# Perceiver kernel: context features copied out raw and rectified later, exponential's table loaded behind the logarithm, three feature buffers

## The chip, the cores and the metric

One Trainium2 chip, one core. The metric is the device time of one execution in microseconds (us), lower is better. All data is float32 unless said otherwise.

## What is computed

The reference runs four layers of a small perceiver on a latent array `x` of 2 batches x 256 tokens x 256 features, with a context `ctx` of 2 x 4096 x 256. The change touches two cross attentions to the context (layers 0 and 1) and a third one (layer 3). Cut to what matters:

```
# layers 0 and 1: masked softmax attention to the context, 16 heads of 16
q, k, v = heads(h @ Wq), heads(ctx @ Wk), heads(ctx @ Wv)
x = x + merge(softmax(mask(q @ k.T / 4)) @ v)

# layer 3: linear attention on "focused" features
def focus(x, factor):
    x = abs(where(x >= 0, x, 0.01 * x)) + 1e-6
    return softmax(log(x) * factor, axis=-1) * x.mean(axis=-1)
def sparsify(x):          # within each head of 16 features, keep the 11 largest
    return x * (rank(x) < 11)
k = sparsify(focus(ctx @ Wk.T)); q = sparsify(focus(h @ Wq.T))
y = (q @ (k.T @ v)) / (q @ k.mean(axis=1) + 1e-6)
```

The focused features of the context, `sparsify(focus(ctx @ Wk.T))`, and their sums `k.T @ [ctx, 1]` do not depend on `x`. The kernel works them out early, in the gaps of the two context attentions: batch 0 within layer 0's, batch 1 within layer 1's.

## The kernel before

Class `ContextAttention` does one context attention. Its work is cut into 8 units (`UNITS`: a batch and a group of 4 heads), each of `PER` = 16 rounds. The loop in `attend` (L944) runs over rounds `g` and issues, in this order: `first_scores` (L1070: scores of a unit against a half of 512 keys and 128 queries, of which VectorE takes the maximum at L1088); the round's *fill* (L962), some work chosen ahead by the planner; a few steps of VectorE's ranking of features (L963 to L967); `scores` (L1094) of the unit before, with its maximum already subtracted, in two PSUM pairs that ScalarE turns into weights by two exponentials (L1114); `weigh` (L1117), PE's product of the weights of one round earlier with the values; and the steps of a chunk's weighing (L976). PE, VectorE and ScalarE run strictly in the order of the program (`manual_schedule`), so whatever is issued first on an engine is in front of what follows. PSUM holds three pairs for the scores (`sc=3`), one bank for all fills (`mm=1`) and one for the weighed sum (`acc=1`).

A fill is one of: keys (L991), values (L1033), one or two tiles of 128 tokens of the context's features (`Focus.project`, L721), half of the sums of a chunk (`add_up`, L745), a unit's shift of the queries or its normalization. Class `Focus` (L584) treats the context in 8 chunks of 4 tiles:

- `project` multiplies a tile with the weights into the PSUM bank and calls `magnitudes` (L604) for each tile. That runs two Relus on ScalarE, straight from PSUM, with scales 1 and -0.01, into the chunk's buffer `y` (tile `fy`, of which there are 2) and into `low` (1 buffer), each with the row's total as an accumulator. POOL adds the two (L611).
- `weigh` (L613) is a generator of five parts: a logarithm of the whole chunk (L618) and POOL's product with the factor (L619); the maximum on VectorE (L621); four exponentials in two parts (L624); small factors (L629 to L632). Logarithm and exponential use different tables of ScalarE; the compiler puts a table load ahead of an activation whose table isn't there. Relu and copy need none.
- `sparsify` (L640) ranks the features by 15 comparisons, 47 parts in all, the first ones long (960 elements a partition) and the last ones short (64), and ends with POOL's scaling by the factors (L665).
- `add_up` multiplies the chunk with the context's tokens on PE.

`plan` (L835) decides all of it ahead, step by step, by a list `todo` of (deadline, earliest, which). In each round without a fixed fill it takes the first that is ready in order of deadline. Features come in pairs of tiles where time is short (`pressed`, L895). Chunk `kc`'s features may be planned once the sums of `kc - 2` are. When the last tile of a chunk is planned in round g, its weighing is put at rounds g+1, g+3, g+4, g+5 and g+6 (L920), and round g+2 is marked in `logs`: nothing but sums, or work that is due, is planned there (L886), so that round is often empty. The ranking may begin at g+7. `credit` paces the ranking by VectorE's estimated free time in a round (2.0 us, or 2.75 with a fill of eight matmuls, less what is `taken`), by the costs at L634.

In layer 3, `l3_xattn` (L1776) calls `magnitudes` (L1814), with a scale by row, and `weigh` (L1816) for the query's features, outside of any plan.

Of the kernel before, what the change touches and what calls it, by code (L numbers as in the profile page):

```python
# [19 lines left out]
F32 = mybir.dt.float32  # L20
BF16 = mybir.dt.bfloat16
I32 = mybir.dt.int32
AF = mybir.ActivationFunctionType
# [3 lines left out]
P = 128  # L27
# [556 lines left out]
class Focus:  # L584
# [19 lines left out]
    def magnitudes(self, pool, y, total, t, ps, scales=(1.0, -0.01)):  # L604


        nc = self.nc
        low = pool.tile([P, D], F32, tag="low", name="low", bufs=1)
        for i, (out, scale) in enumerate(zip((y[:, t, :], low), scales)):
            nc.scalar.activation(out, ps, AF.Relu, scale=scale, accum_out=total[:, i, t : t + 1])  # L610
        nc.gpsimd.tensor_tensor(y[:, t, :], y[:, t, :], low, ALU.add)  # L611

    def weigh(self, y, total, factor):  # L613


        nc = self.nc
        top, norm = (self.net.sm(NT, name=n, tag=n) for n in ("f_top", "f_norm"))
        nc.scalar.activation(y, y, AF.Ln, bias=self.eps)  # L618
        nc.gpsimd.tensor_scalar(y, y, self.power[:, 0:1], 1.0, ALU.mult, ALU.mult)  # L619
# [12 lines left out]
        nc.vector.tensor_tensor(factor, factor, norm, ALU.mult)  # L632
# [61 lines left out]


    def start(self, b, pool):
        self.b, self.pool, self.chunks, self.ctx, self.weighing = b, pool, [], [], []
# [23 lines left out]
    def project(self, kc, first, n=1):  # L721

        net, nc = self.net, self.nc
        if first == 0:
            y = self.pool.tile([P, NT, D], F32, name="fy", tag="fy")
# [15 lines left out]
        for i in range(n):  # L741
            self.magnitudes(self.pool, y, total, first + i, ps[:, i * D : (i + 1) * D])
        yield

    def add_up(self, kc, m):  # L745

# [14 lines left out]
class ContextAttention:  # L761
# [73 lines left out]
    def plan(self):  # L835
# [24 lines left out]
        for kc in range(NKC):  # L860
            first = 5 + 31 * kc // 2
            todo += [(first + 2 * t + 4, first + t, ("features", kc, t)) for t in range(NT)]
            todo += [(first + 30 + m, first + 14, ("sums", kc, m)) for m in range(ND)]
        for j in range(self.begun, n * NKC // 2):


# [15 lines left out]
        ranked, at = 0, 0  # L882

        def ready(g, deadline, earliest, which):
            kind, kc, *_ = which
            if earliest > g or (g in logs and kind != "sums" and deadline > g):  # L886
                return False
            if kind == "keys":

                return kinds.get(g - 1) != kind or deadline <= g  # L890
            if kind == "features":
                return kc < 2 or not any(w[:2] == ("sums", kc - 2) for _, _, w in todo)
            return kind != "sums" or over.get(kc, g) + 1 < g

        def pressed(g):  # L895
# [6 lines left out]
        for g in range(STEPS):  # L902
            room = short
            t = None if g in fills else next((t for t in todo if ready(g, *t)), None)
            if t is not None:
                todo.remove(t)
                kind, *which = t[2]
                kinds[g] = kind
                assert t[0] >= g or kind in ("features", "sums"), (g, t)
                fills[g] = make[kind](*which)  # L910
                if kind == "features":
                    kc, tile = which
                    if tile + 1 < NT and pressed(g):
                        todo.remove(next(t for t in todo if t[2] == ("features", kc, tile + 1)))
                        fills[g] = focus.project(kc, tile, 2)
                        room, tile = full, tile + 1
                    if tile == NT - 1:


                        for behind in (0, 2, 3, 4, 5):  # L920
                            self.weighings.setdefault(g + 1 + behind, []).append(kc)
                        logs.add(g + 2)
                        taken[g + 3] += 1.22
                        taken[g + 6] += 0.65
                        begin[kc] = g + 7
                else:
                    room = full
                    taken[g] += 0.42 * (kind == "sums")
            if g < PER:
                room = 0.5  # L930
            if g >= last + 1:
                room = 2.2
            credit = min(credit, 0.5) + room - taken[g]
# [10 lines left out]
    def attend(self, vpool, ppool, fpool):  # L944
# [12 lines left out]
        for g in range((n + 1) * PER + LAG + 2):  # L957
# [9 lines left out]
                run(rankings[kc], 1)  # L967
            if 0 <= second < n * PER:
                self.scores(second // PER, second % PER)
            if 0 <= second - 1 < n * PER:  # L970
                self.weigh((second - 1) // PER, (second - 1) % PER)
            if g in self.done:
# [1229 lines left out]
```

## Time and profile before

| | us |
|---|---|
| median of three runs | 2561.95 (2557.09 to 2562.78) |
| the profiled execution, whole | 2563.84 |
| its span, first to last instruction | 2562.1 |
| PE, VectorE (DVE), ScalarE (ACT), POOL busy | 2343.6, 1558.8, 1054.6, 355.6 |
| rounds with first and second scores, layer 0 | from about 90 to 650 |
| the same, layer 1 | from about 1022 to 1586 |
| table loads at L618 (17) and at L1114 (14), each | 1.28 |

The profile is one execution. A line of the timeline gives the start in us, the duration, the engine, the line of the kernel, the operation, what it writes and reads, the shapes, and in brackets the idle time of the engine ahead of it and what ended that. PEld is PE's loading of weights. Float32 matmuls count as two each. An ACTIVATION_READ_ACCUMULATOR follows each ScalarE instruction that writes a total. Lines of DVE, ACT or POOL in a group are followed by their count (x2).

### The profile page before, as it was taken

How to read it: one execution, taken by the hardware profiler on the slowest of the kernel's cores; microseconds unless marked ns; L12 is line 12 of the kernel's file. 1: busy time of each engine (PE TensorE's matmuls, PEld its weight loads, DVE VectorE, ACT ScalarE, POOL GpSimd, SP SyncE). 2: the span in 40 equal slices, each digit the busy share in tenths (PEclk: the TensorE clock that was granted, in tenths of full speed). 3: DMA queues.
4: the chain of work that ended last, by engine and by line, in shares of the span. 5: the costliest groups of instructions: out<-in, count | busy, mean ns of one | idle time of the engine just before them, and what ended most of it. 6: DMA issues, size and time to landing. Idle time of an engine off the chain costs nothing.

```text
span 2562.1 us, 42559 instructions
## 1 busy us (share of the span) xinstructions
PE 2343.6 (91%) x17006; PEld 1247.1 (49%) x17014; DVE 1558.8 (61%) x2702; ACT 1054.6 (41%) x1830; POOL 355.6 (14%) x523
## 2 busy tenths in 40 slices
PE   7999999999998579999999999989999996789998
PEld 3454545544544354544555544554448453345453
DVE  4968897779546468888878878243331254335252
ACT  2455555555616132555555555431131252223141
POOL 3000010000034612100011000000020031003030
PEclk9999999999989789999999999988999897898989
DMA  5432223231010133232222220202222100000100
GB/s 191 137 97 80 93 88 94 71 107 43 10 55 17 47 107 108 91 95 95 94 88 82 83 76 26 81 14 61 87 89 88 42 18 14 33 21 12 56 12 21
DMA packets 97797, 174.40 MB, mean 68 GB/s; under 512 B 15120, under 2 KB 63888, under 8 KB 96704
## 3 DMA queue, kind: packets, MB, share of 16 engines
q1 hardware_dynamic: 97600, 171.68, 20.7%
q8 instruction: 135, 2.21, 0.4%
q14 instruction: 62, 0.51, 0.1%
HBM read 154.25 MB, written 0.59 MB: 60 GB/s over the span
## 4 chain that ended last, share of the span: by engine, by line
PE 79%; DVE 10%; ACT 5%; issue 3%; POOL 2%; DMA 1%; SPq 0%; ACTq 0%; DVEq 0%; POOLq 0%
PE s L1080 11%; PE s L1104 10%; PE attn_acc L1128 9%; PE v_ps L180 6%; PE proj L180 6%; PE k_ps L1001 4%; DVE mx L1088 3%; PE kc_sum L180 2%; PE expert L180 2%; PE s L180 2%; PE c_acc L1666 2%; PE f_ps L180 2%; PE ffn_ps L180 2%; PE s L1402 2%; PE o L411 1%
## 5 line engine op out<-in xcount | busy, mean ns | idle before, releaser
L1088 DVE TENSOR_REDUCE mx<-s 128x2 f32<-128x1024 f32 x512 | 603.5, 1220 | 206.3 <-PE s L1080 203.6
L1114 ACT ACTIVATE p<-s 128x1024 f32<-128x1024 f32 x512 | 496.3, 1021 | 237.9 <-PE s L1104 235.8
L1104 PE MATMUL s<-xa_q,xa_k 32*128 32x256 f32 x4096 | 339.0, 403 | 22.9 <-DVE mx L1088 20.8
L1080 PE MATMUL s<-xa_k,xa_q 32*128 32x512 f32 x2048 | 345.3, 639 | 7.6 <-ACT p L1114 3.6
L1104 PEld LDWEIGHTS s<-xa_q,xa_k 32*128 32x128 f32 x4096 | 211.8, 184 | 160.5 <-issue 98.5
L1128 PE MATMUL attn_acc<-p,xv 128*32 128x256 f32 x4096 | 277.1, 387 | 0.9 <-ACT p L1114 0.9
L1080 PEld LDWEIGHTS s<-xa_k,xa_q 32*128 32x128 f32 x2048 | 116.4, 183 | 128.9 <-issue 58.7
L654 DVE TENSOR_TENSOR ge<-fy 128x960 bf16<-128x960 f32 (+14 forms) x240 | 172.9, 720 | 6.2
L1128 PEld LDWEIGHTS attn_acc<-p,xv 128*32 128x32 f32 x4096 | 107.5, 109 | 132.2 <-issue 85.5
L611 POOL TENSOR_TENSOR fy<-fy,low 128x256 f32<-128x256 f32 x64 | 50.4, 787 | 793.1 <-ACT low L610 793.1
L656 DVE TENSOR_TENSOR rank<-rank,ge 128x960 bf16<-128x960 bf16 (+14 forms) x240 | 111.4, 464 | 6.0
L658 DVE TENSOR_TENSOR rank<-rank,ge 128x960 bf16<-128x960 bf16 (+14 forms) x240 | 105.6, 440 | 2.7
L387 POOL TENSOR_SCALAR p<-p,r 128x128 f32<-128x128 f32 (+1 forms) x192 | 82.7, 444 | 140.2 <-DVE r L383 80.0
L1048 ACT COPY xv<-v_ps 128x512 f32<-128x512 f32 x64 | 37.6, 588 | 142.8 <-PE v_ps L180 133.0
L368 ACT ACTIVATE p<-p,top 128x256 f32<-128x256 f32 (+1 forms) x128 | 57.1, 447 | 42.7 <-DVE top L356 40.2
L180 PE MATMUL f_ps<-f_wk,f_ctx 128*128 128x256 f32 x256 | 70.0, 401 | 1.2 <-ACT low L610 1.2
L1001 PE MATMUL k_ps<-ctx_k,w_L0x_wq 128*64 128x512 f32 x256 | 65.1, 615 | 2.6 <-DMA ctx_k<-in_ctxT 2.2
L1666 PE MATMUL c_acc<-pT,ctx_n 128*128 128x256 f32 x256 | 63.1, 392 | 4.2 <-ACT pT L1639 3.0
L180 PEld LDWEIGHTS f_ps<-f_wk,f_ctx 128*128 128x128 f32 x256 | 44.1, 189 | 46.8 <-issue 27.3
L233 ACT ACTIVATE sq<-xc 128x512 f32<-128x512 f32 x24 | 14.7, 630 | 125.8 <-DVE xc L232 125.8
L180 PE MATMUL v_ps<-w_L0x_wv,ctx_v 128*128 128x256 f32 x256 | 63.8, 392 | 0.8 <-ACT k_dense L1014 0.8
L180 PE MATMUL kc_sum<-f_tok,fy 128*128 128x257 f32 x256 | 64.2, 393 | 0.0
(458 smaller groups left out, 3365.1 us busy)
## 6 DMA issues: line engine op xcount, KB each, us to landing
ctx_k<-in_ctxT SPq DMA_DIRECT2D x128, 512.0 KB
ctx_v<-in_ctxT SPq DMA_DIRECT2D x64, 256.0 KB
xa_k<-k_dense SPq DMA_DIRECT2D x512, 32.0 KB
f_ctx<-in_ctxT SPq DMA_DIRECT2D x32, 256.0 KB
f_tok<-in_ctx SPq DMA_DIRECT2D x16, 512.0 KB
ctxT<-in_ctxT SPq DMA_DIRECT2D x16, 512.0 KB
ctx_n<-in_ctx SPq DMA_DIRECT2D x16, 512.0 KB
xa_k<-key_masks SPq DMA_DIRECT2D x128, 8.0 KB
```

Of the source, the lines that this page charges most:

```text
L180: self.nc.tensor.matmul(out, lhsT=lhsT, rhs=rhs, start=i == 0, stop=i == len(pairs) - 1)
L387: nc.gpsimd.tensor_scalar(p[:, j, :nk], p[:, j, :nk], r[:, j : j + 1], 1.0, ALU.mult, ALU.mult)
L654: nc.vector.tensor_tensor(ge[:, :, :n], w[:, :, :n], w[:, :, P - n :], ALU.is_ge)
L656: nc.vector.tensor_tensor(rank[:, :, P - n :], rank[:, :, P - n :], ge[:, :, :n], ALU.add)
L658: nc.vector.tensor_tensor(rank[:, :, :n], rank[:, :, :n], ge[:, :, :n], ALU.subtract)
L1001: nc.tensor.matmul(ps[i * HR : (i + 1) * HR, :], lhsT=self.wk[:, d, c * HR : (c + 1) * HR], rhs=ctx[:, d, :], start=d == 0, stop=d == ND - 1,)
L1080: nc.tensor.matmul(pairs[i // 2][:, i % 2, :], lhsT=self.q[u][rows, qt * P : (qt + 1) * P], rhs=k[rows, :], start=True, stop=True,)
L1088: nc.vector.tensor_reduce(mx[:, qt, 2 * i : 2 * i + 2, kc], sc, AX.X, ALU.max)
L1104: nc.tensor.matmul(pairs[i // 2][:, i % 2, kk * S : (kk + 1) * S], lhsT=k[rows, at], rhs=self.q[u][rows, :], start=True, stop=True,)
L1114: nc.scalar.activation(p, sc, AF.Exp, scale=DH**-0.5)
L1128: nc.tensor.matmul(self.acc[i * HP : (i + 1) * HP, :S], lhsT=v[:, 2 * k2 + kk, at : at + HP], rhs=ps[i // 2][:, i % 2, kk * S : (kk + 1) * S],
L1666: nc.tensor.matmul(accs[m], lhsT=of[:, (k + i) % (KC // P), m * P : (m + 1) * P], rhs=pT[:, i, :], start=k + i == 0, stop=k + i == KT - 1,)
```

## The change

`project` copies the raw products of its one or two tiles from PSUM into `y` by one ScalarE copy, and notes the tiles in `taken`. A new method `magnitudes_of_taken` runs the Relus from `y`, `low` first and then `y` in place; `attend` calls it behind `scores`, so behind the round's exponentials. `low` has two buffers and `fy` three; features of chunk `kc` may be planned once the sums of `kc - 3` are. In `weigh`, an exponential of one column (`ready`) stands directly behind the logarithm. The planner no longer sets a chunk's weighing at once: it keeps the chunk in `waiting` until sums are planned in some round, or until the ranking of the chunk before is over or has 30 of its parts planned; from there the distances of the weighing's parts and the ranking are as before. The sums' deadline is half a round earlier.

```
@@ -605,9 +605,9 @@
         nc = self.nc
-        low = pool.tile([P, D], F32, tag="low", name="low", bufs=1)
-        for i, (out, scale) in enumerate(zip((y[:, t, :], low), scales)):
-            nc.scalar.activation(out, ps, AF.Relu, scale=scale, accum_out=total[:, i, t : t + 1])
+        low = pool.tile([P, D], F32, tag="low", name="low", bufs=2)
+        for i, out in ((1, low), (0, y[:, t, :])):
+            nc.scalar.activation(out, ps, AF.Relu, scale=scales[i], accum_out=total[:, i, t : t + 1])
         nc.gpsimd.tensor_tensor(y[:, t, :], y[:, t, :], low, ALU.add)
     def weigh(self, y, total, factor):
@@ -616,6 +616,9 @@
         nc = self.nc
         top, norm = (self.net.sm(NT, name=n, tag=n) for n in ("f_top", "f_norm"))
         nc.scalar.activation(y, y, AF.Ln, bias=self.eps)
+
+        ready = self.net.sm(1, name="ready", tag="ready")
+        nc.scalar.activation(ready, self.eps, AF.Exp)
         nc.gpsimd.tensor_scalar(y, y, self.power[:, 0:1], 1.0, ALU.mult, ALU.mult)
         yield
         nc.vector.tensor_reduce(top, y, AX.X, ALU.max, negate=True)
@@ -694,7 +697,7 @@
     def start(self, b, pool):
-        self.b, self.pool, self.chunks, self.ctx, self.weighing = b, pool, [], [], []
+        self.b, self.pool, self.chunks, self.ctx, self.weighing, self.taken = b, pool, [], [], [], []
         self.loads = iter([(kc, i) for kc in range(NKC) for i in range(2)])
         self.tokens = pool.tile([P, NT, D + 1], F32, name="f_tok", tag="f_tok", bufs=1)
@@ -722,7 +725,7 @@
         net, nc = self.net, self.nc
         if first == 0:
-            y = self.pool.tile([P, NT, D], F32, name="fy", tag="fy")
+            y = self.pool.tile([P, NT, D], F32, name="fy", tag="fy", bufs=3)
             total = net.sm(2, NT, name="f_total", tag="f_total")
             factor = net.sm(NT, name="f_factor", tag="f_factor")
             self.chunks.append((y, total, factor))
@@ -738,9 +741,15 @@
             ctx = self.ctx[kc * 2 + t // 2]
             at = slice(t % 2 * P, (t % 2 + 1) * P)
             net.matmuls(ps[:, i * D : (i + 1) * D], [(ctx[:, d, at], self.wk[:, d, :]) for d in range(ND)])
-        for i in range(n):
-            self.magnitudes(self.pool, y, total, first + i, ps[:, i * D : (i + 1) * D])
+
+        nc.scalar.copy(y[:, first : first + n, :], ps[:, : n * D].rearrange("p (t d) -> p t d", t=n))
+        self.taken += [(y, total, first + i) for i in range(n)]
         yield
+
+    def magnitudes_of_taken(self):
+        for y, total, t in self.taken:
+            self.magnitudes(self.pool, y, total, t, y[:, t, :])
+        self.taken = []
     def add_up(self, kc, m):
@@ -860,7 +869,7 @@
         for kc in range(NKC):
             first = 5 + 31 * kc // 2
             todo += [(first + 2 * t + 4, first + t, ("features", kc, t)) for t in range(NT)]
-            todo += [(first + 30 + m, first + 14, ("sums", kc, m)) for m in range(ND)]
+            todo += [(first + 29.5 + m, first + 14, ("sums", kc, m)) for m in range(ND)]
         for j in range(self.begun, n * NKC // 2):
@@ -879,7 +888,17 @@
         make = dict(keys=self.project_keys, values=self.project_values, features=focus.project, sums=focus.add_up)
         self.weighings, self.rankings, costs = {}, {}, focus.costs()
         begin, over, logs, credit = {}, {}, set(), 0.0
-        ranked, at = 0, 0
+        ranked, at, waiting = 0, 0, []
+
+        def take_logs(g):
+
+            kc, _ = waiting.pop(0)
+            for behind in (0, 2, 3, 4, 5):
+                self.weighings.setdefault(g + behind, []).append(kc)
+            logs.add(g + 1)
+            taken[g + 2] += 1.22
+            taken[g + 5] += 0.65
+            begin[kc] = g + 6
         def ready(g, deadline, earliest, which):
             kind, kc, *_ = which
@@ -889,7 +908,7 @@
                 return kinds.get(g - 1) != kind or deadline <= g
             if kind == "features":
-                return kc < 2 or not any(w[:2] == ("sums", kc - 2) for _, _, w in todo)
+                return kc < 3 or not any(w[:2] == ("sums", kc - 3) for _, _, w in todo)
             return kind != "sums" or over.get(kc, g) + 1 < g
         def pressed(g):
@@ -915,21 +934,19 @@
                         fills[g] = focus.project(kc, tile, 2)
                         room, tile = full, tile + 1
                     if tile == NT - 1:
-
-
-                        for behind in (0, 2, 3, 4, 5):
-                            self.weighings.setdefault(g + 1 + behind, []).append(kc)
-                        logs.add(g + 2)
-                        taken[g + 3] += 1.22
-                        taken[g + 6] += 0.65
-                        begin[kc] = g + 7
+                        waiting.append((kc, g))
                 else:
                     room = full
                     taken[g] += 0.42 * (kind == "sums")
+
+                    if kind == "sums" and waiting and waiting[0][1] < g - 1:
+                        take_logs(g - 1)
             if g < PER:
                 room = 0.5
             if g >= last + 1:
                 room = 2.2
+            if waiting and waiting[0][1] < g and (ranked == waiting[0][0] or ranked + 1 == waiting[0][0] and at >= 30):
+                take_logs(g)
             credit = min(credit, 0.5) + room - taken[g]
             while ranked < NKC and begin.get(ranked, STEPS) <= g and credit > 0.3:
                 self.rankings.setdefault(g, []).append(ranked)
@@ -967,6 +984,7 @@
                 run(rankings[kc], 1)
             if 0 <= second < n * PER:
                 self.scores(second // PER, second % PER)
+            focus.magnitudes_of_taken()
             if 0 <= second - 1 < n * PER:
                 self.weigh((second - 1) // PER, (second - 1) % PER)
             if g in self.done:
```

More of the change, by code (lines that the diff above doesn't have):

```diff
@@ L607, in magnitudes @@
         nc = self.nc
-        low = pool.tile([P, D], F32, tag="low", name="low", bufs=1)
-        for i, (out, scale) in enumerate(zip((y[:, t, :], low), scales)):
-            nc.scalar.activation(out, ps, AF.Relu, scale=scale, accum_out=total[:, i, t : t + 1])
+        low = pool.tile([P, D], F32, tag="low", name="low", bufs=2)
+        for i, out in ((1, low), (0, y[:, t, :])):
+            nc.scalar.activation(out, ps, AF.Relu, scale=scales[i], accum_out=total[:, i, t : t + 1])
         nc.gpsimd.tensor_tensor(y[:, t, :], y[:, t, :], low, ALU.add)
@@ L618, in weigh @@
         nc.scalar.activation(y, y, AF.Ln, bias=self.eps)
+        ready = self.net.sm(1, name="ready", tag="ready")
+        nc.scalar.activation(ready, self.eps, AF.Exp)
         nc.gpsimd.tensor_scalar(y, y, self.power[:, 0:1], 1.0, ALU.mult, ALU.mult)
@@ L696, in start @@
     def start(self, b, pool):
-        self.b, self.pool, self.chunks, self.ctx, self.weighing = b, pool, [], [], []
+        self.b, self.pool, self.chunks, self.ctx, self.weighing, self.taken = b, pool, [], [], [], []
         self.loads = iter([(kc, i) for kc in range(NKC) for i in range(2)])
@@ L724, in project @@
         if first == 0:
-            y = self.pool.tile([P, NT, D], F32, name="fy", tag="fy")
+            y = self.pool.tile([P, NT, D], F32, name="fy", tag="fy", bufs=3)
             total = net.sm(2, NT, name="f_total", tag="f_total")
@@ L740, in project, with magnitudes_of_taken @@
             net.matmuls(ps[:, i * D : (i + 1) * D], [(ctx[:, d, at], self.wk[:, d, :]) for d in range(ND)])
-        for i in range(n):
-            self.magnitudes(self.pool, y, total, first + i, ps[:, i * D : (i + 1) * D])
+        nc.scalar.copy(y[:, first : first + n, :], ps[:, : n * D].rearrange("p (t d) -> p t d", t=n))
+        self.taken += [(y, total, first + i) for i in range(n)]
         yield
+    def magnitudes_of_taken(self):
+        for y, total, t in self.taken:
+            self.magnitudes(self.pool, y, total, t, y[:, t, :])
+        self.taken = []
     def add_up(self, kc, m):
@@ L862, in plan @@
             todo += [(first + 2 * t + 4, first + t, ("features", kc, t)) for t in range(NT)]
-            todo += [(first + 30 + m, first + 14, ("sums", kc, m)) for m in range(ND)]
+            todo += [(first + 29.5 + m, first + 14, ("sums", kc, m)) for m in range(ND)]
         for j in range(self.begun, n * NKC // 2):
@@ L881, in plan, with take_logs @@
         begin, over, logs, credit = {}, {}, set(), 0.0
-        ranked, at = 0, 0
+        ranked, at, waiting = 0, 0, []
+        def take_logs(g):
+            kc, _ = waiting.pop(0)
+            for behind in (0, 2, 3, 4, 5):
+                self.weighings.setdefault(g + behind, []).append(kc)
+            logs.add(g + 1)
+            taken[g + 2] += 1.22
+            taken[g + 5] += 0.65
+            begin[kc] = g + 6
         def ready(g, deadline, earliest, which):
@@ L891, in ready @@
             if kind == "features":
-                return kc < 2 or not any(w[:2] == ("sums", kc - 2) for _, _, w in todo)
+                return kc < 3 or not any(w[:2] == ("sums", kc - 3) for _, _, w in todo)
             return kind != "sums" or over.get(kc, g) + 1 < g
@@ L917, in plan @@
                     if tile == NT - 1:
[L920 to L925, printed above, removed]
+                        waiting.append((kc, g))
                 else:
@@ L928, in plan @@
                     taken[g] += 0.42 * (kind == "sums")
+                    if kind == "sums" and waiting and waiting[0][1] < g - 1:
+                        take_logs(g - 1)
             if g < PER:
@@ L932, in plan @@
                 room = 2.2
+            if waiting and waiting[0][1] < g and (ranked == waiting[0][0] or ranked + 1 == waiting[0][0] and at >= 30):
+                take_logs(g)
             credit = min(credit, 0.5) + room - taken[g]
@@ L969, in attend @@
                 self.scores(second // PER, second % PER)
+            focus.magnitudes_of_taken()
             if 0 <= second - 1 < n * PER:
```

## The prediction

> **What bounds the kernel now.** I read the chain of waits first, then the two stretches in which the changed code runs, then single steps in the timeline.
>
> ```profile
> PE 79%; DVE 10%; ACT 5%; issue 3%; POOL 2%; DMA 1%; SPq 0%; ACTq 0%; DVEq 0%; POOLq 0%
> ```
>
> ```profile
> 90.00:650.00 560.00, 545.35 (x5116) 278.94 (x5116) 459.79 (x645) 306.08 (x458) 49.29 (x68) 1.00 0.26 84
> 1022.00:1586.00 564.00, 548.73 (x5132) 280.93 (x5132) 458.74 (x643) 303.73 (x458) 48.59 (x68) 0.99 0.26 83
> ```
>
> The second fence gives the two middle stretches of the context attentions (start:end, length, then busy us of PE, PE's loads, DVE, ACT and POOL). ScalarE is busy for 306 of 560 us, so it has room on average. It matters only where its queue is momentarily late. A step is the distance between the first L1080 matmuls of successive rounds in the timeline, and it comes in two kinds. With a fill of eight matmuls (keys, values, sums) it takes 5.24 to 5.31 us and PE is full. With one feature tile, a transpose of the maxima or no fill it takes 4.52 us whatever PE has to do: the first scores, their maximum, the second pair of scores and the weighing follow each other through three PSUM pairs. So a single feature tile costs no more than an empty step, and I look for gain only in steps above these two values.
>
> The first such kind is a step with two feature tiles:
>
> ```profile
> 265.68 1.15 PE L1104 MATMUL s<-xa_q,xa_k 32*128 32x256 f32 x16
> 265.83 0.38 ACT L610 ACTIVATE fy<-f_ps 128x256 f32<-128x256 f32 x1 [2.28 <-issue]
> 266.81 0.89 POOL L611 TENSOR_TENSOR fy<-fy,low 128x256 f32<-128x256 f32 x1 [26.70 <-ACT low L610]
> 267.15 1.37 DVE L654 TENSOR_TENSOR ge<-fy 128x768 bf16<-128x768 f32 x1
> 267.74 0.38 ACT L610 ACTIVATE low<-f_ps 128x256 f32<-128x256 f32 x1 [0.70 <-POOL fy L611]
> 268.11 1.93 ACT L1114 ACTIVATE p<-s 128x1024 f32<-128x1024 f32 x2
> 268.26 0.52 PEld L180 LDWEIGHTS sums<-den,a 128*128 128x128 f32 x4 [0.92 <-ACT low L610]
> ```
>
> Four Relus run ahead of the exponentials, the last one waits 0.70 us for the one `low` tile, the exponentials start at 268.11, and PE waits 0.92 us because the Relus still hold the single mm bank. The second kind follows a logarithm:
>
> ```profile
> 152.32 1.15 ACT L618 ACTIVATE fy<-fy,eps 128x1024 f32<-128x1024 f32 x1
> 154.36 1.28 ACT L1114 ACT_TABLE_LOAD   x1 [0.90 <-PE s L1104]
> 155.66 1.94 ACT L1114 ACTIVATE p<-s 128x1024 f32<-128x1024 f32 x2
> ...
> 223.14 1.15 ACT L618 ACTIVATE fy<-fy,eps 128x1024 f32<-128x1024 f32 x1
> 224.30 1.28 ACT L1114 ACT_TABLE_LOAD   x1
> 225.60 1.94 ACT L1114 ACTIVATE p<-s 128x1024 f32<-128x1024 f32 x2
> ...
> 229.76 0.59 ACT L1048 COPY xv<-v_ps 128x512 f32<-128x512 f32 x1 [2.23 <-PE v_ps L180]
> ```
>
> At 154.36 (a step with sums) the load of exponential's table waits 0.90 us for scores that it doesn't need. At 224.30 (an empty step) it already stands directly behind the logarithm. The step after takes 6.58 and 6.49 us, against 5.30 normally: 1.2 to 1.3 us are lost, the time that the exponentials were late. The copy at 229.76 shows 2.23 us of idle ScalarE behind a step's exponentials.
>
> **What the Trainium skill says.** "ScalarE: Activation LUTs", section "What ACT_TABLE_LOAD costs", gives 1283 ns for a load, 186 ns + 0.833 ns an element for an ACTIVATE with immediates, 93 ns more for each pointer operand, and an overlap of 93 ns between neighbours. The trace agrees: 1283 ns, and 384 ns for the Relu of 256 elements (399 by the formula). It adds a drain of about 1380 ns to a load; here the logarithm starts 0.02 us behind its load, so I count none. Its section "Table sets: the hidden batching unit" has relu and copy in every set; no load stands at L610, so Relus and copies may go anywhere. "GPSIMD Engine Reference", section "1. Specifications", says that POOL contends with DVE instructions that have two SBUF inputs: the `ge` of 768 at 267.15, beside POOL's add, took 1.37 us, against 0.96 us at 657.93 with POOL idle.
>
> **The change, part by part** (minus is faster).
>
> *Copy and late Relus, two tiles.* ScalarE now makes one copy of 128x512 (0.59 us, the row of L1048) before the exponentials. It ends at 265.83 + 0.59 = 266.42; the scores would allow the exponentials at 266.93 (1.25 us behind L1104's start, as at 317.40 and 318.64). So it is hidden, as a value fill's is. The Relus move behind the exponentials and read SBUF. No row shows that: the floor is 0.38 us (PSUM, L610), the ceiling 0.51 (L624, SBUF with a pointer bias). I take 0.41, four are 1.65 us and fit into the 2.23 us idle; at the ceiling 2.04 still do. POOL's add moves along; its queue has nothing urgent. Steps with two tiles and a denominator in the middle stretches take 6.35, 6.51, 6.48, 6.34, 6.51, 6.47 us; the same with keys takes 5.78 (at 181.96, 511.05). That is 0.57 + 0.73 + 0.70 + 0.56 + 0.73 + 0.69 = 3.98. Two more, at 103.21 and 1035.27, delay their successors to 6.27 and 6.22 against 5.30: 1.89. Sum **-5.9**. A single tile gains nothing: its step is at 4.52 with the Relus in it.
>
> *First phase* (no second scores). Here the Relus hold the mm bank:
>
> ```profile
>   PEld sums L180: 6.1, 6
>   PEld f_ps L180: 4.3, 4
> ```
>
> The first row is already in the 5.9. Of the 4.3 us in the second, VectorE's maxima, which run nearly without a gap from 53.9 to 67.9 and from 991.2 to 1000.5, let through about what DVE idles: 0.9 in the first attention (of 1.04 us idle at 63.24), 0.3 in the second. **-1.2**.
>
> *The small exponential.* The same instruction at L955:
>
> ```profile
> L955 ACT ACTIVATE ready<-eps x2: 203/204/204, 26.4 to 965.2; 128x1 f32<-128x1 f32 x2
> ```
>
> In an empty step it removes nothing and adds 0.11 to 0.20 us in front of the exponentials; I take 0.15. In a step with sums the load moves from 154.36 to the logarithm's end at 153.47, and the exponentials from 155.66 to about 154.95: -0.7.
>
> *The log's place and three buffers.* A log now waits until the ranking before it has 30 of its 47 parts planned, or is over, or until sums come. Followed by hand with the planner's own costs, 30 parts are 20.2 of 26.1 us of ranking. Chunk 1 finds its ranking over: same place, beside sums, in both layers. For chunks 2, 3, 4 and 7 the ranking has 20 to 29 parts when the tiles are done, so the logs go one to three steps later; chunk 5 goes one later, and its step, which had sums at 463.38, becomes empty; chunk 6 stays. I find no log that moves onto sums: those of the chunk before come only when its ranking is over, and those of two before are done by then. So in each layer 5 logs with work behind them lie in empty steps, and the log of chunk 7, with empty steps behind it, costs nothing now (4.55 at 623.03). That gives 10 x 0.15 = **+1.5** and 2 x 0.7 = **-1.4**. Moving an empty step changes nothing in the sum, since the number of steps and fills is fixed. The third buffer only allows the delay. Rankings of chunks 2 to 4 shift by two or three steps, and nothing waits for them; sums of the last chunk come three or four steps later in the tail, where the last ranking would end near 682 and POOL's factors near 684, against PE reaching those sums near 687: hidden by 3 us. The half step in the sums' deadline only changes ties. No DMA and no SP instruction is added; a feature load goes out when its tile is planned, as before.
>
> *The query's features (L1814)* share the code. `low` comes first and needs `low_rstd`, ready 0.21 us after `rstd`: **+0.2**. The small exponential stands there behind a load that POOL and DVE cover (2150.10 to 2152.59).
>
> Sum: -5.9 - 1.2 + 1.5 - 1.4 + 0.2 = **-6.8 us**. The profiled execution took 2563.84 us, 1.7 more than its span, and would take 2557.0. It lies 1.9 us above the median of the three runs, 2561.95, so the forecast is 2561.95 - 6.8 = 2555.2, written as 2555.
>
> **Rivals.**
> 1. *Logs meet sums.* If the planner puts the ten logs beside sums after all, each loses the 0.15 and gains 0.7: 8.5 us more, 2547. For it: the diff has a branch for it. Against: the order of the rankings, above.
> 2. *Cover gone.* Relus, adds on POOL and the copy total more work than before on ScalarE (0.37 us a tile for the copy, 0.06 for SBUF). If these delay the next fill's copy, or the planner makes more pairs of tiles (each costs 5.3 + 4.52 in place of 2 x 4.52, 0.8 us), four or five of either eat 4 us: 2559.
> 3. *Slower: logs at the ranking's end.* At 1306.93 a step took 6.73 us instead of 4.52, because a ranking's many short last parts pushed the maxima back (DVE's maxima at 1308.83, 1.32 us of PE idle). The delayed logs bring POOL's product (1.12 us) and its contention to exactly there, with the maximum of 1.21 us soon after. There are ten delayed logs; 2.2 us for each that collides; from the fourth on the change loses, and six give 13.2 - 6.8 = +6.4: 2568. Against it: the planner books the 1.22 us, and of 16 ranking ends now only one stalls so.
>
> **How the numbers follow.** Chances: forecast 0.50 (own range 2551 to 2559), rival 1 0.12, rival 2 0.22, rival 3 0.16. About 0.2%, 5 us, is what a measurement of this kernel can tell from no change. Beyond -5 us lie some 0.36 of the forecast and all of rival 1: faster 0.48. The rest of the forecast and nearly all of rival 2 are the same, 0.34; rival 3 and a little of rival 2 slower, 0.18. The range is 2546 to 2566: from rival 1 to just short of rival 3's six, leaving some 0.1 on each side at most.
>
> **What would show it.** Right: steps with two tiles at 5.8 us with a denominator, no ScalarE wait on POOL at the `low` Relu, nobody but the next fill waiting for the copy, Relus near 0.41 us behind the exponentials, the load behind every logarithm without a wait, and the step after an empty log step near 6.6. Wrong: logs beside sums in most rounds (rival 1), more pairs of tiles or a fill's copy late behind Relus (rival 2), steps of 6 us and more at ranking ends with PE waiting for the maxima (rival 3).

## The result and the profile after

| us | before | after |
|---|---|---|
| median (5 runs each, side by side) | 2561.95 (2553.83 to 2567.34) | 2546.58 (2544.49 to 2548.88) |
| profiled execution, its span | 2563.84, 2562.1 | 2544.49, 2542.8 |
| ScalarE, VectorE, POOL busy | 1054.6, 1558.8, 355.6 | 1083.0, 1544.8, 352.1 |
| the two attentions together | 1320.8 | 1313.0 |
| PE at half clock, all in all | 243.3 | 219.8 |

The ratio is 0.9953, with a 95% interval of 0.9935 to 0.9971: 12 us faster, give or take 5 (the two medians stand 15.4 apart). Run again among the experiments (as after_again, 7 runs) the changed kernel took 2552.67 us, ratio 0.9965 (0.9948 to 0.9981). "The two attentions together" is the distance from the first first-scores matmul to the last second-scores matmul, in both context layers, in the profiled execution. Between two executions these stretches agree to 0.3 us (1320.8 and 1321.1 for the kernel before) where PE's clock is the same in them, so single steps can be compared there. "At half clock" is the length of all spells in which the trace's clock record says 0.5.

The line of engines from the chain of waits, after; VectorE, ScalarE and PE stand almost where they stood:

```profile
PE 80%; DVE 10%; ACT 5%; issue 2%; POOL 1%; DMA 1%; SPq 0%; ACTq 0%; DVEq 0%; POOLq 0%
```

The two middle stretches after (start:end, length, busy us of PE, PE's loads, DVE, ACT, POOL, then clock and DMA). ScalarE has gained 14 us of work in the first and 12 in the second (copies, more expensive Relus, small exponentials), and has still 240 us to spare:

```profile
90.00:650.00 560.00, 545.76 (x5156) 279.51 (x5158) 448.26 (x639) 319.80 (x488) 46.42 (x68) 0.99 0.27 85
1015.00:1572.00 557.00, 542.53 (x5104) 276.38 (x5100) 448.48 (x632) 315.40 (x487) 46.30 (x68) 1.00 0.27 84
```

A step with two feature tiles, after, from the timeline (the same chunk as the one shown before):

```profile
265.26 0.59 ACT L745 COPY fy<-f_ps 128x512 f32<-128x512 f32 x1 [2.23 <-PE f_ps L180]
266.23 1.07 PE L1146 MATMUL attn_acc<-p,xv 128*32 128x256 f32 x16
266.40 1.94 ACT L1132 ACTIVATE p<-s 128x1024 f32<-128x1024 f32 x2 [0.55 <-PE s L1122]
267.23 0.52 PEld L180 LDWEIGHTS sums<-den,a 128*128 128x128 f32 x4 [0.41 <-issue]
268.22 0.42 ACT L610 ACTIVATE low<-fy 128x256 f32<-128x256 f32 x1
```

Before, the exponentials began 2.28 us behind the first Relu and PE's denominators waited 0.92 us for a Relu. Now the copy is done in 0.59 us, the exponentials wait for nothing but their scores, PE's pause ahead of the denominators is 0.41 us of issue, and the Relus run behind. The step takes 5.83 us instead of 6.35.

The logarithms, after: one beside sums (first four lines), one in an empty step (the rest):

```profile
142.27 1.15 ACT L618 ACTIVATE fy<-fy,eps 128x1024 f32<-128x1024 f32 x1
143.43 1.28 ACT L621 ACT_TABLE_LOAD   x1
144.73 0.20 ACT L621 ACTIVATE ready<-eps 128x1 f32<-128x1 f32 x1
144.84 1.92 ACT L1132 ACTIVATE p<-s 128x1024 f32<-128x1024 f32 x2
```

```profile
222.53 1.15 ACT L618 ACTIVATE fy<-fy,eps 128x1024 f32<-128x1024 f32 x1
223.70 1.28 ACT L621 ACT_TABLE_LOAD   x1
224.99 0.20 ACT L621 ACTIVATE ready<-eps 128x1 f32<-128x1 f32 x1
225.10 1.92 ACT L1132 ACTIVATE p<-s 128x1024 f32<-128x1024 f32 x2
```

The wait of 0.90 us ahead of the load is gone in the first, and the step behind it takes 5.79 us instead of 6.58. In the second the load stood directly behind the logarithm before, too; all that is new is the small instruction, which puts the exponentials 0.11 us behind the load's end where they began 0.02 behind it.

### The profile page after: what moved, and what is told of

It reads as the page before. It is cut to its first block, busy times and chain, and to the rows that moved or that the text cites. A ratio compares the mean times of both kernels' runs of the same rounds, so it can differ in the third digit from the quotient of the medians.

```text
span 2542.8 us, 42543 instructions
## 1 busy us (share of the span) xinstructions
PE 2326.5 (91%) x17014; PEld 1237.4 (49%) x17014; DVE 1544.8 (61%) x2702; ACT 1083.0 (43%) x1898; POOL 352.1 (14%) x523
## 4 chain that ended last, share of the span: by engine, by line
PE 80%; DVE 10%; ACT 5%; issue 2%; POOL 1%; DMA 1%; SPq 0%; ACTq 0%; DVEq 0%; POOLq 0%
PE s L1098 11%; PE s L1122 11%; PE attn_acc L1146 9%; PE v_ps L180 6%; PE proj L180 5%; PE k_ps L1019 4%; DVE mx L1106 3%; PE f_ps L180 3%; PE expert L180 2%; PE kc_sum L180 2%; PE s L180 2%; PE c_acc L1684 2%; PE ffn_ps L180 2%; PE s L1420 2%; PE o L411 1%
## 5 line engine op out<-in xcount | busy, mean ns | idle before, releaser
L1098 PE MATMUL s<-xa_k,xa_q 32*128 32x512 f32 x2048 | 337.5, 641 | 6.2 <-issue 2.8
L611 POOL TENSOR_TENSOR fy<-fy,low 128x256 f32<-128x256 f32 x64 | 46.4, 726 | 875.5 <-ACT fy L610 875.2
L659 DVE TENSOR_TENSOR rank<-rank,ge 128x960 bf16<-128x960 bf16 (+14 forms) x240 | 104.2, 434 | 6.0
L661 DVE TENSOR_TENSOR rank<-rank,ge 128x960 bf16<-128x960 bf16 (+14 forms) x240 | 100.9, 420 | 2.6
```

The source lines that it names most:

```text
L659: nc.vector.tensor_tensor(rank[:, :, P - n :], rank[:, :, P - n :], ge[:, :, :n], ALU.add)
L661: nc.vector.tensor_tensor(rank[:, :, :n], rank[:, :, :n], ge[:, :, :n], ALU.subtract)
L1098: nc.tensor.matmul(pairs[i // 2][:, i % 2, :], lhsT=self.q[u][rows, qt * P : (qt + 1) * P], rhs=k[rows, :], start=True, stop=True,)
```

## The experiments

Each was timed beside the kernel before. "Attentions" is as above. A third number, "at 220 us", takes out the clock: over 242 runs of all these kernels I fitted one value for each kernel and one common slope to the time at half clock, worked out as 2 x (1 - mean granted clock) x time. The slope is 0.42 us for each us at half clock; the scatter left is 2.2 us, and the standard error of a kernel's value is 0.4 to 1.1 us, so differences of 1 or 2 us in this column are not clear of noise.

| kernel | median us (runs) | ratio (95%) | attentions | at 220 us |
|---|---|---|---|---|
| before, beside the three sets | 2561.6, 2561.8, 2561.8 (59, 12, 28) | | 1320.8 | 2554.5 to 2555.6 |
| control | 2562.32 (22) | 1.0002 (0.9993 to 1.0012) | 1321.1 | 2555.0 |
| relus_only | 2542.06 (6) | 0.9937 (0.9920 to 0.9954) | 1307.2 | 2543.5 |
| exp_only | 2554.72 (22) | 0.9979 (0.9969 to 0.9989) | 1318.1 | 2552.1 |
| plan_only | 2563.64 (22) | 1.0014 (1.0003 to 1.0024) | 1326.7 | 2562.6 |
| after, after_again | 2546.58 (5), 2552.67 (7) | 0.9953, 0.9965 | 1313.0, 1316.0 | 2545.9, 2542.9 |
| no_exp | 2544.60 (6) | 0.9941 (0.9926 to 0.9955) | 1310.5 | 2543.4 |
| early_relus | 2577.04 (6) | 1.0063 (1.0049 to 1.0077) | 1330.3 | 2561.0 |
| held_sums | 2537.42 (6) | 0.9916 (0.9899 to 0.9934) | 1305.2 | 2535.3 |
| relus_exp | 2547.60 (14) | 0.9965 (0.9943 to 0.9988) | 1307.9 | 2544.9 |
| self_wait | 2548.64 (6) | 0.9940 (0.9920 to 0.9961) | 1308.6 | 2543.0 |
| half_round | 2548.92 (13) | 0.9958 (0.9941 to 0.9976) | 1310.4 | 2544.4 |
| held_no_exp | 2552.44 (8) | 0.9948 (0.9930 to 0.9966) | 1307.2 | 2540.6 |

### The parts alone

**control** is the kernel before, unchanged.

> The kernel before, unchanged, profiled once more. Theory A (the change gains about 10 us inside the two context attentions, and the other 9 us between the two profiles are spells in which the clock of PE happened to be granted at one half): a ratio of 1.000 within 0.2%, middle stretches of the attentions again near 540 us each apart from such spells, and the stretch behind the second attention anywhere between 923 and 934 us. Theory B (the code behind the attentions really runs faster in the changed kernel): that stretch again at 932 us, within 2.

It shows what a measurement can tell: 2562.32 against 2561.57, and attentions that differ by 0.3 us. The stretch behind the second attention took 931.9 us, as it did before (932.0), so it does not decide between the two theories.

**relus_only**: the kernel before with the copy, the late Relus and two `low` buffers; old planner, no small exponential.

```
-        for i in range(n):
-            self.magnitudes(self.pool, y, total, first + i, ps[...])
+        nc.scalar.copy(y[:, first : first + n, :], ps[...])
+        self.taken += [(y, total, first + i) for i in range(n)]
...
                 self.scores(second // PER, second % PER)
+            focus.magnitudes_of_taken()
```

> The kernel before with the raw copy, the late Relus and two low buffers alone; planner, two feature buffers and logarithm as before. Theory A: -5.9 us in the middle stretches (steps of two tiles with a denominator at 5.8 instead of 6.4 to 6.5, the successors of the two others at 5.3), -1 in the first phase, so about -7 us, ratio 0.997. Rival (the gain is the planner's): below -2 us here.

Attentions 13.9 us shorter than control's: more than the whole change. The plan is the same, so the steps can be set side by side. Six steps with two tiles and a denominator: 6.35 to 6.51 became 5.83 or 5.84, -3.65 in all; the two successors: 6.27 and 6.22 became 5.30, -1.89. That is -5.5 where I had -5.9. Not foreseen: the four steps behind logs with sums fell from 6.52 or 6.58 to 5.64 or 5.70, -0.88 each, -3.5 in all, without a small exponential. (The rest of the 13.9: the first phase -1.3, the steps around half-clock windows in the second attention -1.5, and a little in many full steps.) The log of that step, from the timeline of ScalarE:

```profile
148.43 1.15 ACT L618 ACTIVATE fy<-fy,eps 128x1024 f32<-128x1024 f32 x1
149.60 1.28 ACT L1120 ACT_TABLE_LOAD   x1
150.89 1.94 ACT L1120 ACTIVATE p<-s 128x1024 f32<-128x1024 f32 x2
```

The load follows the logarithm at once. The semaphores that the trace has with each instruction of ScalarE explain it. Before, then relus_only, at this place:

```
L618  ACTIVATE fy<-fy,eps   [waits for POOL]
L1114 EVENT_SEMAPHORE       [waits for PE]
L1114 ACT_TABLE_LOAD
L1114 ACTIVATE p<-s         [waits for ScalarE]
...
L618  ACTIVATE fy<-fy,eps   [waits for POOL]
L1120 ACT_TABLE_LOAD
L1120 ACTIVATE p<-s         [waits for PE]
```

Before, the exponential has two waits: for PE's scores, and for ScalarE itself (its own earlier writes). One stays on the exponential; the other becomes an instruction of its own, an EVENT_SEMAPHORE, and that stands ahead of the load, so the load waits too. A late Relu works in place on what ScalarE has just written, so it waits for ScalarE itself; an exponential behind it needs only PE, and the load is free. The number of such instructions at the exponentials falls (views of L1114 before, of L1120 in relus_only):

```profile
L1114 ACTq EVENT_SEMAPHORE  x456: 17/17/17, 119.0 to 1630.6; - x152
L1120 ACTq EVENT_SEMAPHORE  x328: 17/17/17, 104.9 to 1615.3; - x164
```

**exp_only**: the kernel before with the small exponential.

```
         nc.scalar.activation(y, y, AF.Ln, bias=self.eps)
+        ready = self.net.sm(1, name="ready", tag="ready")
+        nc.scalar.activation(ready, self.eps, AF.Exp)
```

> The kernel before with the small exponential behind the logarithm alone. Theory A: the steps behind the four logs beside sums lose about 0.75 us each (6.55 becomes 5.8), those behind empty log steps gain 0.05 each: about -2.7 us, ratio 0.999. Rival (the small exponential is only one more instruction): +1 to +2 us.

The two middle stretches became 1.30 and 1.35 us shorter. The four steps behind logs with sums fell by 0.79, 0.89, 0.79 and 0.78; each step behind an empty log step grew by 0.09; but for one of 0.14 no other step of the middle stretches moved by more, save those around the two half-clock windows. The attentions explain 3.0 of the 6.9 us between the medians; at equal clock the gain is 3 us.

**plan_only**: the kernel before with the changed planner, and three `fy` buffers.

> The kernel before with the new planner and three feature buffers alone; Relus from PSUM ahead of the exponentials, no small exponential. Theory A: logs of chunk 6 go beside sums, of chunk 5 into an empty step, and sums of chunk 6 move out of the tail of the first attention, but the log steps still cost 1.2 us each and there are more pairs of tiles, each 0.7 us dearer: between -2 and +2 us, ratio 1.000. Rival (the gain is the planner's): -5 us or more.

Attentions 5.6 us longer, though no half-clock window fell into them and two fall into control's: the planner alone costs 7 to 8 us, where I had between -2 and +2. The plan has more pairs of tiles: rounds 6, 7, 20, 51, 67, 69, 83 of the first attention instead of 6, 20, 51, 67, 83, and 6 and 69 more in the second. A pair is dear as long as the Relus are early. At round 69, timeline:

```profile
359.98 0.38 ACT L610 ACTIVATE low<-f_ps 128x256 f32<-128x256 f32 x1
361.94 0.38 ACT L610 ACTIVATE low<-f_ps 128x256 f32<-128x256 f32 x1 [1.13 <-POOL fy L611]
362.32 1.93 ACT L1122 ACTIVATE p<-s 128x1024 f32<-128x1024 f32 x2
363.38 0.30 PEld L1088 LDWEIGHTS s<-xa_k,xa_q 32*128 32x128 f32 x4 [1.51 <-ACT p L1122]
```

The second `low` waits 1.13 us for POOL, the exponentials are late, PE's next first scores wait 1.51 us for them: a successor of 6.81 us (6.45 in the second layer), where the changed kernel with its late Relus has 5.18.

**early_relus**: the changed kernel, with `magnitudes_of_taken` called right behind the fill, ahead of the exponentials.

```
             run(fills.get(g, ()))
+            focus.magnitudes_of_taken()
...
-            focus.magnitudes_of_taken()
```

> The changed kernel with the Relus, still from the raw copy, ahead of the exponentials. Theory A (what counts is that the exponentials come first): steps of two tiles lose what they had won, 12 or 13 of them at about 1.2 us (copy 0.59 and four Relus of 0.37 to 0.42 in front, against 2.28 with the wait for low): +8 to +15 us against the changed kernel, so slower than relus from PSUM. Rival (what counts is that the bank is free early and that there are two low buffers): +2 us or less.

Attentions 17.4 us longer than after (I had 8 to 15), the time slower than before. The step with two tiles is 5.83 us here as well, because the copy alone frees the bank. But the exponentials stand behind the Relus (the two-tile step at 265.88, timeline):

```profile
269.82 0.42 ACT L610 ACTIVATE low<-fy 128x256 f32<-128x256 f32 x1
271.30 0.42 ACT L610 ACTIVATE fy<-fy 128x256 f32<-128x256 f32 x1
271.72 1.92 ACT L1132 ACTIVATE p<-s 128x1024 f32<-128x1024 f32 x2
272.77 0.30 PEld L1098 LDWEIGHTS s<-xa_k,xa_q 32*128 32x128 f32 x4 [0.77 <-ACT p L1132]
```

So the loss moves into the following steps: 6.66 instead of 5.30 at 111.34, 5.65 instead of 5.02 at 281.00, and 5.4 instead of 5.1 behind most single tiles. The copy and two `low` buffers do not pay without the order. Two things stay open: late Relus straight from PSUM, without the copy, were not run, and part of the loss may be VectorE's, since 51 of POOL's 68 adds at L611 overlap a step of the ranking here, against 3 in the changed kernel.

### Why the parts do not add

**no_exp**: the changed kernel without the small exponential.

> The changed kernel without the small exponential. Theory A: steps behind the four logs beside sums 0.75 us longer (5.8 becomes 6.55), those behind empty log steps 0.05 shorter: +2.5 us against the changed kernel. Rival (it only costs): -1 to -2 us.

Not slower: attentions 2.5 us shorter than after, 2.2 of them in a step of the first phase that waits for a transfer. Against after_again the comparison is exact: 12 steps behind logs are shorter here by 0.08 or 0.09 each, 1.1 us, and nothing else moved by over 0.04 in the middle stretches, save one step with a half-clock window in after_again. That fits the reading of relus_only: the late Relus keep the load from being late, and the small exponential only costs. Six of the 14 loads do have the wait for scores ahead of them here, but four of them lie in empty steps, where the scores are there in time (0.02 us), and two near the end (0.10 and 0.13 us).

**relus_exp**: relus_only and the small exponential.

> Old planner, raw copy and late Relus, and the small exponential. If the gains of the Relus and of the small exponential are separate terms (the first run of each: -6.0 and -6.9 in the two middle stretches for the Relus, -1.3 and -1.3 for the exponential), the middle stretches are 1.3 us shorter each than with the Relus alone. If they are the same gain (the table load loses its wait for the scores either way: the Relus, reading and writing in place, make ScalarE wait for itself, after which the exponentials need only one wait, so that none is left to hang on the load), the steps behind the logs with sums stay at 5.7 to 5.8 us, the small exponential only adds 0.09 us behind each log, and the middle stretches are 0.6 us longer each than with the Relus alone. Time 2541 to 2544 us then; 2539 us if the terms are separate.

The same gain, twice. Eleven of the steps behind logs are 0.08 or 0.09 us longer than in relus_only; none is shorter on that account. Attentions +0.7, at equal clock +1.4, which is not clear of noise. The time I gave, 2541 to 2544 us, was missed (2547.60); its runs were at half clock for longer.

**self_wait**: the kernel before with one instruction more in each round, which does nothing but wait for ScalarE. (`mark` is one column, set once ahead of the rounds.)

```
                 self.scores(second // PER, second % PER)
+                nc.scalar.activation(mark, mark, AF.Relu)
```

> The kernel before, with one more ScalarE instruction behind each round's exponentials: a Relu of one column in place, which does no useful work and only makes ScalarE wait for its own earlier instruction. If it is that wait which frees the table load from the scores, the four steps behind the logs with sums fall from 6.5 to about 5.7 us (-0.88 each, 3.5 us in all), the steps with two tiles stay at 6.35 to 6.51 us, and the time is 2558 us. If the free load comes from something else in the late Relus, the steps behind the logs stay at 6.5 us, and the time is that of before or up to 2 us more (0.2 us a round on ScalarE, mostly hidden).

```profile
151.62 1.15 ACT L618 ACTIVATE fy<-fy,eps 128x1024 f32<-128x1024 f32 x1
152.78 1.28 ACT L1117 ACT_TABLE_LOAD   x1
154.08 1.94 ACT L1117 ACTIVATE p<-s 128x1024 f32<-128x1024 f32 x2
```

The load is free, and the four steps fell by 0.79, 0.99, 0.79, 0.79 us: 3.4, as expected. Five of the six two-tile steps stayed. The cause of the free load is settled; of the EVENT_SEMAPHOREs at the exponentials none is left. But the attentions became 12.5 us shorter than control's, not 3.5, and the forecast of 2558 us was far off. Two things add most to it. No half-clock window lies in these attentions, where control has two; the steps around those were 2.4 us shorter. And nearly every step in which PE is full is 0.05 to 0.12 us shorter (5.21 became 5.09), together some 4.8 us (the rounds behind the last first scores add 1.0): every exponential has one wait now, where 228 of control's 256 rounds have two, and the first of a step begins 1.18 us behind its first score matmul instead of 1.24. This is in the timeline as 0.49 instead of 0.54 us of idle ScalarE ahead of the exponentials. In relus_only 92 of the 256 rounds have one wait, in the changed kernel 88. At equal clock this one instruction gains 12.6 us, about as much as the whole change. Whether it would add to the late Relus was not run.

### The planner

**half_round**: relus_only with the sums' deadline half a round earlier.

```
-            todo += [(first + 30 + m, first + 14, ("sums", kc, m)) for m in range(ND)]
+            todo += [(first + 29.5 + m, first + 14, ("sums", kc, m)) for m in range(ND)]
```

> The Relus alone, with the old planner, in which only the sums' deadline is half a round earlier. If the extra pairs of tiles of the changed plan come from that half round, this plan has pairs in rounds 6, 7, 20, 51, 67, 69, 83 of the first attention (before: 6, 20, 51, 67, 83) and 6 and 69 more in the second; each pair in the middle costs 0.8 to 1.3 us, the first phases become 1 to 2 us longer each, and the time is 3 to 5 us above that of the Relus alone, 2545 to 2547 us. If the delay of the logs makes the new plan dear instead, this one costs nothing, and the time is 2542 us.

The pairs are as expected: it is the half round that makes them, through the count of deadlines in `pressed`. The cost is not: 3.2 us in the attentions, of which 2.7 are one step of 8.52 us with a half-clock window; at equal clock 0.9, not clear of noise. The median, 2548.92 us, is above the 2545 to 2547 that I gave. The pair at round 69 has a successor of 5.18 us here; a pair with late Relus costs 0.55 (5.07 instead of 4.52). That is the interplay: late Relus make pairs cheap.

**held_sums**: the changed kernel, but half of a chunk's sums is kept for the round of the log two chunks later, with a second token buffer.

```
+                held = m == ND - 1 and kc + 2 < NKC
+                todo.append((first + (41 if held else 29.5 + m), first + 14, ("sums", kc, m)))
```

> The changed kernel, with the second half of a chunk's sums held back until the logarithm of the chunk after the next is planned, so that all seven later logs stand beside sums, and two token buffers. Theory A: of the ten logs in empty steps with work behind them each loses 0.7 us (6.5 becomes 5.8), and there are five pairs of tiles fewer at 0.7: -7 to -11 us against the changed kernel, ratio about 0.992. Rival (the place of the log makes no difference, or the held sums and their tokens collide): within 3 us of the changed kernel.

Logs of chunks 1 to 7 lie beside sums now, and 10 rounds are empty instead of 13. The steps behind the logs take 5.5 to 5.8 us (one, in a half-clock window, 7.20), and the median of 2537.42 us beats both kernels (ratio 0.9916, against 0.9953 and 0.9965 of the changed one; at equal clock 7 to 10 us less), although two windows of 6.8 us at half clock fall into its attentions.

**held_no_exp**: the same without the small exponential.

> The kernel with held sums (half of a chunk's sums kept for the round of a log, two token buffers) without the small exponential. All logs but the first and last lie beside sums here. If the Relus free the load from the scores, nothing is lost without the small exponential, 0.09 us is gained behind each of 16 logs, and the time is 2536 us. If here, with scores that come late in every log's round, the load still waits for them in steps whose round before had no Relu (the wait of ScalarE for itself is lacking), up to 0.9 us is lost in each such step, six a layer at most, and the time is 2540 to 2548 us.

```profile
232.50 1.15 ACT L618 ACTIVATE fy<-fy,eps 128x1024 f32<-128x1024 f32 x1
234.54 1.28 ACT L1134 ACT_TABLE_LOAD   x1 [0.89 <-PE s L1124]
235.84 1.94 ACT L1134 ACTIVATE p<-s 128x1024 f32<-128x1024 f32 x2
```

Here the log comes rounds after the last tile, so no Relu stands ahead of it, the second wait is back, and the load waits 0.89 us for scores. Seven steps are longer by 0.76 to 0.95, 5.6 us; at equal clock the kernel is 5.3 us slower than held_sums. The attentions' sums (1307.2 against 1305.2) hide that, as held_sums has the two windows of 6.8 us at half clock in them. The median, 2552.44 us, is above the 2540 to 2548 that I gave; the profiled execution was at half clock for longer than any other but early_relus. So the small exponential has its worth, but in this plan, not in the changed kernel's.

## Why the prediction was right, and where not

The side was right. The median lies 0.6 us above the lower end of the range and 8.6 us below the forecast, and that it lies inside is partly luck: most of the gap between the two profiled executions is not in the attentions, which the sum was about (last paragraph). The sum for the attentions, -7.0 without the query's +0.2, met a measured -7.9; but terms of opposite sign were wrong beneath it. The query's +0.2 came true: its first Relu waits 1.60 us where it waited 1.40.

| term | predicted | measured in the changed kernel |
|---|---|---|
| two-tile steps, their successors | -5.9 | -5.5: 5.83 each; successors 5.30 |
| logs beside sums | -1.4 | -3.6: six steps (below) |
| logs in empty steps | +1.5 | 0.09 each, less than 1 us in all |
| first phases | -1.2 | +2.4 and +1.2 |
| planner | 0 | pairs at round 69: +1.1; in the first attention -1.1 behind the last first scores, +1.2 in the two steps before |
| one wait instead of two | not seen | about -1.6 in relus_only |
| half-clock windows in the attentions | not seen | about +2.0 in the first, -2.5 in the second |

These make about -6; the 2 us that are left are spread over small differences.

**Copy and late Relus.** Mechanism and size held. The Relu from SBUF takes 0.417 us (0.41 taken), only one of the 179 copies of fills stands directly behind a Relu (at 989.7), and early_relus shows that the gain is gone without the order.

**"I find no log that moves onto sums"** failed. Chunk 5's log did become an empty step, but chunk 6's went beside sums in both layers (the steps at 546.79 and 1472.3), because chunk 5's ranking ended earlier than I followed it by hand. The steps behind: 6.58 to 5.79 twice, 6.45 to 5.81 and 6.50 to 5.80; and behind chunk 5's now empty log step 6.52 to 5.97 and 6.36.

**The step on the small exponential** had the right place and the wrong cause. I took it to be the only thing that frees the load; self_wait shows that a wait of ScalarE for itself frees it, as the Relus have, and no_exp that the small exponential only costs. Its price was too high: 0.09, not 0.15. "ScalarE: Activation LUTs", section "What ACT_TABLE_LOAD costs" of the Trainium skill, would have given it: 186 ns plus one element, less the 93 ns by which neighbours overlap, is an estimate of 0.09 us; the trace agrees.

**"The half step in the sums' deadline only changes ties"** failed; half_round shows that it makes the pairs. With late Relus they are cheap in the middle, so rival 2 cost about 1 us there and not 4. In the first phase two pairs in a row bring the fills after them forward, and at 73.03 PE waits for the keys' part of the context to land (1.08 us at the first matmul): a step of 5.20 us instead of 2.94 (4.40 in after_again, 3.04 in no_exp: this wait differs from run to run). So the first phase is 2.4 us longer (1.7 in after_again, 0.5 in no_exp), where I had a gain of 0.9. That gain is real (relus_only's is 1.0 us shorter than before's); the plan loses it and more (half_round's is 3.0 us longer than relus_only's). The third buffer does nothing in this plan: the planner's code gives the same list of fills with two.

**Rival 3's evidence** was half a mistake. The step of 6.73 us at 1306.93 was put down to VectorE's late maximum alone, and a second one, of 6.78 at 1546.04, was not seen. The windows of the trace of before show the clock around the second (the last three columns are clock, DMA share, GB/s):

```profile
1546.00:1549.40 3.40, 2.06 (x20) 1.00 (x20) 3.30 (x6) 1.06 (x2) 0.00 (x0) 1.00 0.55 158
1549.40:1552.90 3.50, 3.50 (x32) 1.45 (x28) 2.12 (x4) 2.58 (x3) 0.00 (x0) 0.51 0.01 4
```

PE was busy for 2.06 of 3.40 us while it waited for maxima, and the next 3.4 us ran at half clock. That fits the Trainium skill, "TensorE: Matmul & The Clock Gate", section "What's actually happening": windows of 3413 ns that run freely, and half rate after an idle one. The clock records agree on the length: spells inside the attentions are 3.413 us, or twice that. On "idle" they differ: in the 14 traces PE was busy for 53 to 76% of the window ahead of each of the 18 spells inside the attentions, and 154 other windows of the same grid with no more than 76% were not followed by one. So a stall of 1.3 us cost about 2.1 here (6.78 against 4.64 after). At 1306.93 it cost less than rival 3 counts: the step behind, which follows a logarithm, took 5.10 us where its counterpart in the first attention took 6.44, so of the 2.2 us lost 1.3 came back. The delayed logs brought no such stall in the middle stretches after. The change has one instead in the first attention, where its first phase now ends with more waiting (PE idle for 1.94 of 12.20 us from 84.20 on, against 1.26 of 12.60 from 84.80 on before):

```profile
85.00:96.40 11.40, 9.46 (x56) 4.03 (x50) 11.30 (x16) 1.59 (x3) 0.00 (x0) 0.99 0.52 161
96.40:105.00 8.60, 8.60 (x52) 4.71 (x50) 7.31 (x9) 3.13 (x5) 0.00 (x0) 0.62 0.21 60
```

The step at 96.43 took 8.53 us instead of 5.79.

**The measured gain beyond the attentions.** Of the 19.3 us between the two spans, 7.9 lie in the attentions and 11.4 outside them, where the change touches nothing but the query's features. 23.5 us less at half clock, times the fitted 0.42, is an estimate of 9.9 us of it. But after_again, with 250.1 us at half clock, still takes 6.3 us less outside the attentions than before, and there the clock gives no reason. Of that run I had expected that the stretch behind the second attention is as before, or else 7 us shorter; it was 2.9 us shorter (929.1 against 932.0), which is neither. Over the 14 profiles the part outside varied between 1229.8 and 1244.8 us, so how much of the 11.4 is chance stays open. At equal clock the changed kernel is 9 to 12 us faster than before, and relus_only alone 11. Why one execution of the same kernel has 24 spells at half clock and another 26 stays open: stalls may lie differently to freely running windows, but no run here shows that.

## What to carry to other kernels

Look at which waits the compiler gives an activation before you price a table load: if an activation has two, one of them may stand ahead of the load in front of it. An instruction of the same engine, shortly before, that has already waited for the engine itself can take the second wait away. Drain PSUM with one plain copy and put the elementwise work behind what the other engines wait for; then test each part alone and all pairs, since here two parts bought the same 3.5 us, and one made the other's cost small. In a planner that counts deadlines, a change of half a round is a change of plan: run it and list what it chose.

## What the runs showed that was not expected

- A second wait on an exponential costs 0.06 us of start (1.24 against 1.18 us behind the first score matmul), in nearly every full step.
- A us at PE's half clock goes with 0.42 us more time of this kernel. The Trainium skill, "TensorE: Matmul & The Clock Gate", section "Terms", puts the penalty at the time times (1 - K/N), half of it. It is a little less here, perhaps because PE sometimes waits anyway; no run shows that.
- POOL's adds hardly meet VectorE's ranking any more: of the 68 at L611, 54 overlapped a step of it before and 3 do after. The longest took 1.34 us before and 0.73 after, and VectorE's busy time fell by 14 us though its work is the same.
